# One graph-network kernel of four layers: the last V groups of each layer in one go, V one score group sooner in layer 3, and two small moves on ScalarE's queue

## The chip, the cores and the metric

The kernel runs on one NeuronCore of one Trainium2 chip. The metric is the device time of one execution in microseconds (us); the median of three runs is used. The engines are named as in the profile: PE (TensorE, matmuls and transposes), PEld (its weight loads), DVE (VectorE), ACT (ScalarE), POOL (GpSimd, which here issues the indirect DMAs) and SP (SyncE, which issues plain loads). ACTq, SPq and POOLq are the queues of DMA issues of these engines.

## The reference

x is 3327 x 256 in float32, adj is a 0/1 matrix of 3327 x 3327 in which a row has some 16 ones. Layer 0 is a graph attention with one score per node, a projection and a layer norm. Layers 1 to 3 are transformer blocks whose attention is masked with adj:

```python
qkv = layer_norm(x, g1, be1) @ w_qkv                 # 256 -> 3 x 256
q, k, v = ...                                        # 8 heads of 32
scores = einsum('nhd,mhd->hnm', q, k) * 32 ** -0.5
attn = softmax(where(adj != 0, scores, -inf), axis=-1)
x = x + einsum('hnm,mhd->nhd', attn, v).reshape(n, 256) @ w_proj + b_proj
ff = gelu(layer_norm(x, g2, be2) @ w1 + b1) @ w2 + b2   # 256 -> 1024 -> 256
x = x + ff
```

## The kernel before

Layer 0 reads adj densely, and builds for each node the list of its neighbours. The nodes are sorted by their number of neighbours and cut into 26 blocks of 128 nodes. Block b has CAPS[b] slots (40 for block 0, 24 to 10 for the others); a slot is one neighbour of each of the 128 nodes. From then on attention is sparse.

**Gathers.** Each layer's keys and values lie in DRAM, one row of 512 numbers per node (`kv[L]`). For one slot of one block, POOL issues an indirect DMA that brings the 128 neighbours' rows, one to each partition (L1303 in `issue`). Four slots make a group, the unit of all attention work: 448 slots and about 120 groups per layer. Groups land in a ring of NBUF = 10 tiles. The next group is issued when V of an earlier one has been written down (`values` calls `issue`), and POOL can run it once that V has read its tile.

**Scores.** `scores` (L1325, L1326, both DVE) multiplies k with the block's q and sums over each head. After a block's last group `softmax` subtracts on DVE and takes exp on ACT (L1340). Right behind it `take_q` (L1311) copies the next block's q on ACT.

**V.** `weights` (L1346 to L1353, DVE) makes the softmax weights of a block at its first V group. `values` multiplies v by them (vw, L1366, DVE; three tiles of vw) and adds up over the slots by transposing matmuls into PSUM (L1372, eight rows of PE in the profile for each group). After a block's last V, five short steps follow (`block`): nothing, oT copied by ACT (L1390), projection on PE (L1394, L1396), nothing, residual add on DVE with the statistics for the norm (L1400).

**Chunks.** Blocks are taken in an order that alternates small and large ones, with block 0 last, and are bundled in chunks: three blocks, then fours, then one of two, and block 0 alone. When a chunk's last block is added, `chunk` puts its long steps in a list, each with a cost: norm (rsqrt of 13 small DVE rows, L551 to L582), xn on ACT (L588), transposes (L591), then `up` (L1439), `gelu` on ACT (L1445) and `down` (L1462; L1455 and L1458 for a single block), transposes back (L1476), residual adds (L1480). In layers 1 and 2 the norm and the q/k/v of the next layer follow (`qkv`, L1492), with `keep`, which copies the k/v row (kvr, L1498), scales q (L1499) and writes kvr to DRAM (L1500, ACT's DMA queue). In layer 3 `store` writes the result by an indirect DMA of POOL (L1505).

**Order.** Each engine runs its instructions in the order in which they are written. `Layer.run` writes down one score group, then one or two V groups of an earlier block, then calls `some`. It takes a short step, then long steps as far as a credit goes (raised by `rate` in each call, at most 8), then another short step. After the last score group the remaining ten V groups of block 0 are written, each followed by `some`, and at last what is left of the lists with a rate of 4.

**Between layers.** The next layer's gathers need all 26 kvr writes. In the same stretch SP loads the next layer's weights (`load_rest`, `load_qkv`), each as soon as the last matmul has read the old ones: w_proj, w1 and w2, the bias rows (which DVE splits in three, L1255 to L1259), and w_qkv of the layer after (768 KB, L619; only at the end of layer 1, since layer 3 needs no further one).

Of the kernel before, what the change touches and what calls it, by code (L numbers as in the profile page):

```python
# [8 lines left out]
FP = mybir.dt.float32  # L9
BF = mybir.dt.bfloat16  # L10
I32 = mybir.dt.int32
AF = mybir.ActivationFunctionType
# [5 lines left out]
P = 128  # L18
N = 3327
D = 256  # L20
HEADS = 8
# [502 lines left out]
def sparse_path(ctx, tc, ins, out, dram, flag):  # L524
    nc = tc.nc
    const = ctx.enter_context(tc.tile_pool(name="s_const", bufs=1))
    small = ctx.enter_context(tc.tile_pool(name="s_small", bufs=4))

    ident = const.tile([P, P], FP, name="s_ident")
# [12 lines left out]
    kv = {1: dram.tile([PADDED + 1, KVW[1]], FP, name="kv1"),  # L542
          2: dram.tile([PADDED, KVW[2]], FP, name="kv2"),
          3: dram.tile([PADDED, KVW[3]], FP, name="kv3")}
# [732 lines left out]
    class Layer:  # L1277
# [133 lines left out]
        def chunk(self, blocks, n2):  # L1411
            L, w, nxt = self.L, self.w, self.nxt
# [82 lines left out]
            def keep(j):  # L1495
                b = blocks[j]
                kvr = work.tile([P, 2 * D], FP, tag="kvr", name=f"kvr_{L}_{b}")
                nc.scalar.copy(kvr, c["pk", j])  # L1498
                nc.scalar.mul(t2[:, b, D:2 * D], c["pq", j][:, :D], -HD ** -0.5)  # L1499
                nc.scalar.dma_start(kv[L + 1][b * P:(b + 1) * P, :], kvr)  # L1500

            def store(j):
                b = blocks[j]
# [27 lines left out]
            if nxt is not None:  # L1531
                steps += [at(2, lambda: c["n1"].scale()), *(at(2, t) for t in turns("n1", "n")),
                          at(2, lambda: to_hT("n1", "n", nxt["g1"], nxt["be1"])),
                          at(3, lambda: qkv(0))]
                for j in js:
                    fs = [lambda j=j: keep(j)]
                    if j + 1 < len(blocks):
                        fs.append(lambda j=j: qkv(j + 1))
                    steps.append(at(3, *fs))
            else:  # L1540
                steps += [at(1, lambda j=j: store(j)) for j in js]
# [12 lines left out]
                self.short.pop(0)()  # L1554

        def run(self):
            for _ in range(NBUF):
                self.issue()
            self.take_q(ORDER[0])

            todo, wait = [], {}

            def value():
                if todo[0][1] == 0:
                    self.weights(todo[0][0])
                self.values(*todo.pop(0))

            for k, b in enumerate(ORDER):
                for g in slots[b]:
                    self.scores(*g)  # L1570
                    if g == slots[b][-1]:
                        self.softmax(b)
                        if k + 1 < NB:
                            self.take_q(ORDER[k + 1])
                    for i in wait:
                        wait[i] += 1
                    for _ in range(2 if len(todo) > NBUF // 2 or b == 0 else 1):
                        if todo and wait[todo[0][0]] > 1:
                            value()
                    self.some()  # L1580
                todo += slots[b]
                wait[b] = 0
            while todo:
                value()
                self.some()
            self.rate = 4.0
            while self.short or self.long:
                self.some()
# [45 lines left out]
```

## Time and profile before

| what | us |
|---|---|
| three runs, lowest to highest | 2568.12 to 2575.34 |
| median | 2573.75 |
| profiled execution, its own time | 3158.07 |
| its span | 3156.3 |
| PE, DVE, ACT, POOL busy in the span | 1794.0, 1935.3, 774.6, 1362.7 |
| layer 1: first gather to first gather of layer 2 | 509.5 to 1428.5 |
| layer 2: to first gather of layer 3 | 1428.5 to 2305.9 |
| layer 3: to the end | 2305.9 to 3156.3 |

The profiled execution is much longer than a run without the profiler. Durations of single instructions are read from it; sums of waits are not carried over to the runs without asking. "The tail" of a layer is the stretch from its last gather to the next layer's first, in which POOL has nothing to gather: the last gather of layer 2 ends at 2191.75, the next layer's first starts at 2305.85. The page's mean TensorE clock is 0.735 of full speed.

### The profile page before, as it was taken

The page shows a single profiled execution, that of the slowest core. Times are in us where ns is not written, and L with a number is a line of the kernel's source. Part 1 is how long each engine was busy: PE and PEld are TensorE (multiplying, and loading weights), DVE is VectorE, ACT ScalarE, POOL GpSimd, SP SyncE. Part 2 cuts the span into 40 slices and gives each one's busy share as a digit, 9 for nine tenths or more (in the row PEclk, how much of TensorE's full clock was granted, in tenths as well). Part 3 has the DMA queues.
Part 4 walks back from the last instruction along what each step waited for, and adds up shares of the span by engine and source line. Part 5 has one row for each costly group of instructions (what it writes and reads, how often), then busy time and mean ns, then how long its engine had stood idle before and what let it go on. Part 6 is the DMA issues. An engine that isn't in the chain of part 4 may idle for free.

```text
span 3156.3 us, 24036 instructions
## 1 busy us (share of the span) xinstructions
PE 1794.0 (57%) x7561; PEld 1163.5 (37%) x7561; DVE 1935.3 (61%) x3983; ACT 774.6 (25%) x1316; POOL 1362.7 (43%) x1458
## 2 busy tenths in 40 slices
PE   4767752255666666671457667666713435665556
PEld 3645531133333333350334333433512323433334
DVE  6688995457657656533656756755446556656554
ACT  4455621012222222230112212222300111212112
POOL 4000004545555554305555555544054555565550
PEclk9868766577787886785578778878755766776768
DMA  5334306645555565415455555555064554554560
GB/s 207 131 117 148 129 31 204 174 138 169 165 172 162 156 174 152 112 51 177 141 156 156 163 160 150 175 152 140 24 189 125 156 155 135 169 163 147 161 156 13
DMA packets 144486, 453.80 MB, mean 144 GB/s; under 512 B 29521, under 2 KB 40156, under 8 KB 141021
## 3 DMA queue, kind: packets, MB, share of 16 engines
q0 software_dynamic: 113056, 370.26, 40.9%
q1 hardware_dynamic: 9834, 53.90, 4.9%
q10 hardware_dynamic: 21458, 28.02, 2.5%
q8 instruction: 61, 1.00, 0.1%
q14 instruction: 77, 0.63, 0.1%
HBM read 420.64 MB, written 31.42 MB: 143 GB/s over the span
## 4 chain that ended last, share of the span: by engine, by line
DVE 25%; issue 18%; PE 18%; another core or an unknown queue 17%; POOL 11%; ACT 5%; DMA 5%; DVEq 0%; ACTq 0%; POOLq 0%; SPq 0%
POOL kv L1303 11%; DVE kv L1325 5%; DMA kv<-kv,t 4%; DVE sc L1326 3%; DVE vw L1366 3%; PE pu L1439 3%; PE po L1372 3%; PE py L1462 2%; DVE cand L735 2%; PE pk L1492 1%; PE s_pk L1010 1%; ACT s_aT L724 1%; DVE s_v L731 1%; PE pf L591 1%
## 5 line engine op out<-in xcount | busy, mean ns | idle before, releaser
L1303 POOL DMA_INDIRECT kv<-kv,t x1344 | 1273.0, 947 | 1210.3 <-issue 534.2
L1372 PE MATMUL po<-s_ident,vw 128*128 128x128 f32 x2688 | 475.4, 334 | 580.2 <-DVE vw L1366 387.2
L1372 PEld LDWEIGHTS po<-s_ident,vw 128*128 128x128 f32 x2688 | 395.5, 174 | 724.1 <-issue 373.5
L1325 DVE TENSOR_TENSOR kv<-kv,q 128x1024 f32<-128x1024 f32 (+3 forms) x363 | 413.1, 1138 | 397.1 <-ACT q L1311 274.6
L1366 DVE TENSOR_TENSOR vw<-kv,w 128x1024 f32<-128x1024 f32 x333 | 371.4, 1128 | 87.2 <-remote 84.6
L1326 DVE TENSOR_REDUCE sc<-kv 128x32 f32<-128x1024 f32 (+3 forms) x363 | 414.1, 1141 | 12.4
L1439 PE MATMUL pu<-fT,s_w 128*128 128x512 f32 (+3 forms) x768 | 341.2, 579 | 62.3 <-issue 35.8
L1462 PE MATMUL py<-gT,s_w 128*128 128x512 f32 (+2 forms) x672 | 321.8, 597 | 58.1 <-issue 50.2
L1400 DVE TENSOR_TENSOR t<-t,po 128x256 f32<-128x256 f32 x78 | 32.6, 418 | 390.8 <-remote 254.5
L1445 ACT ACTIVATE gT<-pu,pvb 128x512 f32<-128x512 f32 (+3 forms) x192 | 115.7, 607 | 628.2 <-remote 384.1
L1439 PEld LDWEIGHTS pu<-fT,s_w 128*128 128x128 f32 x768 | 157.4, 222 | 196.1 <-issue 146.4
L1462 PEld LDWEIGHTS py<-gT,s_w 128*128 128x128 f32 x672 | 132.6, 206 | 180.7 <-issue 144.0
L1396 PEld LDWEIGHTS po<-s_w_proj,oT 128*128 128x128 f32 x312 | 71.8, 255 | 281.8 <-issue 272.3
L1394 PE MATMUL po<-bias,s_ones_bf 96*128 96x256 bf16 x78 | 25.2, 324 | 259.7 <-issue 147.4
L1390 ACT COPY oT<-po 128x256 f32<-128x256 f32 x78 | 28.9, 371 | 548.5 <-remote 320.2
L711 POOL MEMSET s_abf<- 128x1 bf16 x23 | 2.2, 104 | 361.4 <-DVE s_v L731 253.7
L1492 PE MATMUL pk<-s_w_qkv,nT 128*128 128x512 f32 x208 | 128.4, 748 | 22.0 <-ACT nT L596 9.9
L735 DVE MAX8 cand<-s_v 128x8 f32<-128x208 bf16 x416 | 118.0, 360 | 0.9
L1396 PE MATMUL po<-s_w_proj,oT 128*128 128x256 f32 x312 | 113.1, 500 | 0.0
L723 PE MATMUL s_ptb<-s_ident_bf,s_abf 128*128 128x128 bf16 x676 | 67.1, 265 | 68.3 <-ACT s_abf L714 45.2
L591 PE MATMUL pf<-s_ident,xn_f 128*128 128x128 f32 x156 | 46.1, 444 | 86.8 <-ACT xn_f L588 66.7
L855 PE MATMUL s_pa<-s_aT,s_hs 128*128 128x256 bf16 x338 | 82.3, 290 | 13.2 <-DVE s_hs L817 13.2
(288 smaller groups left out, 2252.1 us busy)
## 6 DMA issues: line engine op xcount, KB each, us to landing
s_a<-in_adj_dram SPq DMA_DIRECT2D x25, 1663.5 KB
kv<-kv,t POOLq DMA_INDIRECT x1344
kv<-kvr ACTq DMA_DIRECT2D x52, 256.0 KB
kv<-s_kvr ACTq DMA_DIRECT2D x26, 256.0 KB
s_w<-in_L_gnn_w_dram SPq DMA_DIRECT2D x6, 1024.0 KB
t<-ql ACTq DMA_DIRECT2D x6, 592.0 KB
t<-s_x ACTq DMA_DIRECT2D x6, 512.0 KB
s_w_qkv<-in_L_gnn_w_qkv_dram SPq DMA_DIRECT2D x3, 768.0 KB
```

Source lines behind the costliest of these rows:

```text
L735: nc.vector.max(out=self.cand[:, s, :], in_=self.v[:, s, :])
L855: nc.tensor.matmul(self.pa[:, c0:c0 + 2 * P], S.hs[:r, k, :P], aT[:r, k, :], start=(k == 0), stop=(k == NB - 1))
L1303: nc.gpsimd.indirect_dma_start(out=t[:, s, :], out_offset=None, in_=kv[L], in_offset=bass.IndirectOffsetOnAxis(ap=t2[:, b, k:k + 1].bitcas ...
L1325: nc.vector.tensor_mul(k, k, self.q[b][:, None, :].to_broadcast([P, n, D]))
L1326: nc.vector.tensor_reduce(self.sc[b][:, s0:s0 + n, :], k.rearrange("p s (h d) -> p s h d", d=HD), AX.X, ALU.add)
L1366: nc.vector.tensor_mul(vw[:, :n * D].rearrange("p (s h d) -> p s h d", h=HEADS, d=HD), v, self.wp[b][:, s0:s0 + n, :, None].to_broadcast([ ...
L1372: nc.tensor.matmul(self.po[b][:, k * P:(k + 1) * P], vw[:, at:at + P], ident, is_transpose=True, start=(s0 + s == 0 and k == 0), stop=(s0 ...
L1396: nc.tensor.matmul(ps, c["oT"][:, k * P:(k + 1) * P], w["w_proj"][:, k, :], start=False, stop=(k == 1))
L1439: nc.tensor.matmul(c["pu", f][:, :n], w["w1"][:, e, f * P:(f + 1) * P], c["hT"][:, e, :n], start=(e == 0), stop=(e == 1))
L1445: nc.scalar.activation(g[:, :n], c.pop(("pu", f))[:, :n], AF.Gelu_apprx_tanh, bias=w["b1"][:, f:f + 1])
L1462: nc.tensor.matmul(c["py"][e][:, :n], w["w2"][:, f, e * P:(e + 1) * P], g[:, :n], start=(f == 0), stop=last)
L1492: nc.tensor.matmul(ps[:, :c1 - c0], c["hT"][:, e, j * P:(j + 1) * P], nxt["w_qkv"][:, e, c0:c1], start=(e == 0), stop=(e == 1))
```

## The change

There are four edits, in `keep` and in `Layer.run`.

1. In `keep` the DMA that writes the k/v row to DRAM is issued before the scaling of q instead of after it.
2. In layer 3 (the one without `nxt`) a block's V may begin after one score group of the following block instead of two (`behind`).
3. After the last score group, one activation of a 128 x 8 piece of the identity with gelu is issued on ACT, into a tile that nothing reads.
4. The ten V groups that are left are written one after another without `some` between them. What was left of the long steps is written after them, in the old order, with the rate of 4; the chunks stay as they were.

```diff
@@ keep @@
                 nc.scalar.copy(kvr, c["pk", j])
+                nc.scalar.dma_start(kv[L + 1][b * P:(b + 1) * P, :], kvr)
                 nc.scalar.mul(t2[:, b, D:2 * D], c["pq", j][:, :D], -HD ** -0.5)
-                nc.scalar.dma_start(kv[L + 1][b * P:(b + 1) * P, :], kvr)
@@ Layer.run @@
+            L = self.L
...
+            behind = 2 if self.nxt else 1
...
-                        if todo and wait[todo[0][0]] > 1:
+                        if todo and wait[todo[0][0]] >= behind:
                             value()
...
+            table = small.tile([P, HEADS], FP, tag="table", name=f"table_{L}")
+            nc.scalar.activation(table, ident[:, :HEADS], AF.Gelu_apprx_tanh)
             while todo:
                 value()
-                self.some()
             self.rate = 4.0
             while self.short or self.long:
                 self.some()
```

## The prediction

> **What bounds the kernel now.** I read the page's busiest groups first, then POOL's waits, then the chain of waits and the timeline around the three layer ends, and last the table of windows for the granted clock. The page's top group is the gather of keys and values:
>
> ```profile
> L1303 POOL DMA_INDIRECT kv<-kv,t x1344 | 1273.0, 947 | 1210.3 <-issue 534.2
> ```
>
> One gather is 0.947 us busy and, in every unbroken run of them in the timeline, 0.30 us of issue: 1.25 us. A layer has 448, so 560 us; the three take 1680 us of the span. Of the 1210.3 us of idle time, 1344 x 0.30 = 403 are this issue and 116.8 + 114.1 = 231 the two layer changes; 576 us are left, in which POOL waits for a free place in the ring of ten groups. The profiled execution took 3158.07 us (span 3156.3, 1.8 us around it), the median of the three runs is 2573.75: 584 us less. So the unprofiled run has next to no such waits (576 of 584 is an inference from two totals, not a measured row). I take the layers as bound by POOL at 1.25 us a gather, until the last gather has landed, and then by the **tail** of each layer, in which POOL stands still. In the tails the profile has almost none of those waits, so a microsecond saved there is taken off the median one to one.
>
> The tail of layer 1 in the chain of waits, and three of its rows in the timeline:
>
> ```profile
> 1362.27 1.42 PE po L1372 x8
> ...
> 1391.96 4.42 PE po L1372 x40
> 1396.42 1.11 PE po L1372 x8
> ...
> 1418.80 3.20 PE pk L1492 x4
> 1422.00 0.86 PE pq L1492 x4
> 1422.90 4.91 DMA s_w_qkv<-in_L_gnn_w_qkv_dram
> ```
>
> ```profile
> 1402.85 0.60 ACT L588 ACTIVATE xn_f<-t,nm_f,rqy_f 128x256 f32<-128x256 f32 x1 [4.93 <-DVE nm_f L582]
> ...
> 1422.90 0.38 ACT L1499 ACTIVATE t<-pq 128x256 f32<-128x256 f32 x1 [0.28 <-PE pq L1492]
> 1422.91 0.39 ACTq L1500 DMA_DIRECT2D kv<-kvr  x1
> ```
>
> The exp of block 0 ends at 1356.3. V0 is transposed at 1362.3, V1 to V3 sit in gaps of the two-block chunk, V4 to V9 come only after that chunk's last q/k/v matmul (1391.96). Then comes block 0's own chain: oT, projection, add, norm (xn_f at 1402.85), its FFN and its q/k/v. The first gather of layer 2 is at 1428.53. Layer 2's tail repeats this within 0.3 us from exp to xn_f. In layer 3, V-only work is already one stretch of eight:
>
> ```profile
> 3116.22 9.23 DVE L1366 TENSOR_TENSOR vw<-kv,sc 128x1024 f32<-128x1024 f32 x8
> ```
>
> That is 1.154 us a group, DVE's pace.
>
> **What the Trainium skill says.** (1) "TensorE: Matmul & The Clock Gate", "What's actually happening": the array runs at half clock after about 3.4 us of idleness and again at full after about as long a busy stretch. The trace agrees in size: TensorE stands still from 1378.0 to 1383.4, the clock reads 0.50 in 1382 to 1384 and 1.00 from 1388; in the stretch of transposes 3116 to 3126 it stays 1.00. (2) "DMA: Bandwidth & Descriptors", "Queues, rings and completion order": SP and ACT each own a row of rings on the same 16 DMA engines, which serve the rows in turn. The trace agrees: alone, the last kvr write took 2.02 us (layer 2's end, 2300.17); beside the 768 KB of s_w_qkv, asked for in the same 0.01 us, about 4.9. (3) "SBUF — State Buffer", "Who interferes with whom": DVE and GpSimd share a port pair by an exclusive lock. It fits, but doesn't prove, that the first gather follows kvr's landing after 0.7 us in layer 1 and 3.7 in layer 2, amid DVE's bias rows both times. (4) "ScalarE: Activation LUTs", "What ACT_TABLE_LOAD costs": about 1283 ns a load; the rows at L1340 and L1445 show 1283.
>
> **The change, part by part.** Queue order is worked out from `some` and its credits.
>
> *V in one go.* When the scores end, ten V groups and a remainder of the two-block chunk are open: in layers 1 and 2 up2 to up7, down0 to down7, shift, back, norm, q/k/v; in layer 3 only up7, down5 to down7, shift, back, adds, stores. Today the remainder goes between the first V; afterwards V is first, and oT, projection and add of block 0 go among the remainder (two short steps per `some`), while block 0's chunk still follows it ("same chunks"). Layer 1, from V0's end at 1363.69:
> - V1 to V9: there are three vw tiles, so vw3 starts as V0 ends; seven vw at 1.154 = 8.08, plus 1.15 for the last transposes: 1372.92.
> - remainder: 6 up + 8 down at 0.865 = 12.1, projection 1.15: 1386.17. Last down to residual add 1.41 (1376.66 to 1378.07), adds and norm 4.68 (to 1382.75), xn, transposes and nT 2.8: 1395.06.
> - two q/k/v: TensorE is cold here, so the first pk takes the 3.20 of the row above, then 0.86, 1.72, 0.86: 1401.7. After the q copy (0.6) xn_f starts at 1402.3 instead of 1402.85: 0.55 gained. Its norm (13 small DVE rows, 2.6) is done by 1395, hidden behind those matmuls.
> - xn_f now follows matmuls by 1.2 us instead of 4.4 of idleness, so the array is warm: the twelve up matmuls, 2.93 today, become 1.3 (0.11 each, as from 1408 on), and the turn before loses 0.25: 1.8 gained.
>
> So 2.3 us each in layers 1 and 2. Layer 3: V0 ends at 3110.78; V9 at 3110.78 + 8.08 + 1.15 = 3120.0; up7, three down and the projection 4.6; last down to add 1.41; two adds 0.75: block 0's norm starts at 3126.8 instead of 3129.44: 2.65 gained. The last stores on POOL (0.97 each) go with the adds and end long before the final one. No gather is left to issue, so POOL and SP are passed by nothing else; the w_proj load of the next layer merely starts earlier.
>
> *Rows written ahead of q.* For each of 52 keeps the DMA issue (0.33 on ACT's queue) stands ahead of the q copy. The copy waits for pq anyway (0.28), so it is delayed by some 0.1, off the path except for the last. There the write goes at kvr's end, 1422.62 + 0.06, not at 1422.91: 0.2 earlier. In layer 1 that also puts it ahead of s_w_qkv, which is asked for at 1422.90: between 0.2 (still shared) and 3.1 (2.02 from issue to landing as alone). I take 2.2, and 0.2 in layer 2, where no s_w_qkv is loaded. The next thing late is POOL's start after the landing (0.7 or 3.7), unchanged on average, ±3.
>
> *gelu's table.* Nothing. In all three layers a gelu of the two-block chunk stands in ACT's queue between exp and the new instruction (the timeline has the L1445 load at 1358.91 and 3102.80), so the table is already in. The dummy, some 0.2 us, lies in ACT's idle time during V.
>
> *Layer 3, V after one score group.* No instruction is added. The added risk is DVE waiting for exp at `weights`, with score groups behind it. But `take_q` stands after exp on ACT, and the next block's first scores need q: DVE has waited for exp already. So no new wait. V frees its ring place one score group, at most 5 us of POOL, sooner. In the profile POOL's 26 ring waits of layer 3 add up as follows, and could shrink by up to 84 us (at most 5 each):
>
> ```profile
> POOL kv L1303 <- DVE vw L1366: 158.0, 26, 14.4
> ```
>
> Unprofiled there are next to none, so the gain lies between 0 and some 8; as a bound the other way, 3 lost by vw delaying score groups. I take 1.
>
> **Sum:** (2.3 + 2.2) + (2.3 + 0.2) + 2.65 + 1 = 10.65 us, of which 9.65 in the tails; 2573.75 - 10.65 = **2563**. A profiled execution, which has ring waits, could gain several tens more in layer 3.
>
> **Rivals.**
> 1. *The tail is only re-ordered* (0.27): the warm array or the head start of the write doesn't come, or the layer starts draw the longer 3.7 us. Then 0.55 x 2 + 0.4 + 2.65 = 4.15: 2569.6. For it: ahead of warmth only 0.55 us of a 46 us stretch from exp to xn_f is gained, a balance of large terms. Against it: the clock rows. A measurement of this kernel can't tell less than about 0.3% (7.7 us) from no change.
> 2. *The transposes cool the array* (0.10): if V-only work ran at half clock, a group would take the 1.92 us of the slow V3 row (1384.41), and nine take 17.3 instead of 9.2: +8.1 per layer, against gains of 2.3, 2.3 and 2.65; with the writes (2.4) and 1 taken off, +13.6: 2587, slower. It decides from 1.28 us per group on ((9.2 + 2.3) / 9), where layers 1 and 2 break even. Against it: clock 1.00 in layer 3's stretch of eight.
> 3. *Layer 3 had real ring waits* (0.15): 5 to 8 more gained, some 2556. For it: DVE's idle time before kv L1325 is mostly a wait for ACT's q. Against it: 576 of 584.
> 4. *A part does nothing*: so I hold of the table, at no price.
>
> The forecast itself has 0.48. **Numbers.** Predicted 2563. Range 2550 to 2574: rival 3 with the better landings below, rival 1 with noise above (the runs shown span 7 us). Faster by over 0.3%: the forecast, rival 3 = 0.63; same: rival 1, 0.27; slower: rival 2, 0.10.
>
> **What would show it.** In the changed profile: ten vw in a row at 1.15 us after each layer's last exp, clock 1.00 there and in block 0's up matmuls; xn_f of block 0 within 1 us of the last chunk matmul in layers 1 and 2; from exp's end to the next first gather about 67.5 us in layer 1 and 69.5 in layer 2 instead of 72; the last kvr landing 2 to 3 us after its issue in layer 1. Wrong if V takes over 1.28 us a group, if the up matmuls stay cold, or if layer 3's scores start waiting for exp at L1346.

## The result and the profile after

| | us, median | lowest to highest | runs |
|---|---|---|---|
| before (its first three runs and six beside the changed kernel) | 2570.82 | 2565.11 to 2575.34 | 9 |
| changed | 2562.78 | 2560.89 to 2568.05 | 9 |
| changed, second time (a_again) | 2564.56 | 2558.82 to 2567.80 | 12 |
| before, beside the second | 2570.49 | 2566.24 to 2574.38 | 20 |

The ratio is 0.9975 with a 95% interval of 0.9964 to 0.9987, and 0.9973 (0.9965 to 0.9982) the second time. Times the 2570.8 of before that is 6.4 us less (9.3 to 3.3), then 6.9 (9.0 to 4.6); the medians alone lie 8.0 and 5.9 us apart. Forecast were 10.65 us less and 2563. That the predicted time was met to 0.2 us is partly luck: the median of before is 3 us lower here than in its first three runs, and the gain itself was forecast at about one and a half times its measured size.

The profiled execution of the changed kernel took 2567.91 us (span 2566.1), within the range of its other runs. The last experiment, y4, ran on a chip where 20 runs of the kernel before read 3121 us, near the 3158.07 of its first profile, so y4 stands only against those 3121. The length of that first profile most likely came from where it ran, too, and not from being profiled: every other profiled execution took within 6 us of its kernel's median, and y4's profile shows the same long waits for the ring (POOL on vw: 378.3 us in y4, 372.7 in the first profile, 42.3 in the changed kernel). For that reason the kernel before is read below from the profile of e4_table_alone: before plus one idle instruction, span 2567.6.

The page's top group, in the columns of the one shown before (busy us and mean ns | idle before, with its releaser):

```profile
L1303 POOL DMA_INDIRECT kv<-kv,t x1344 | 1273.5, 948 | 642.2 <-issue 334.0
```

The gather costs the same 0.948 us. Of the idle 642.2, 403 are issue and 191 the two layer changes; 48 are left where the first profile had 576.

The tail of layer 1 in the chain of waits (start, length, what); block 0's exp ends at 1132.01:

```profile
1137.96 4.78 PE po L1372 x40
1142.78 1.09 PE po L1372 x8
...
1147.32 1.09 PE po L1372 x8
1148.41 0.87 PE pu L1439 x4
...
1169.60 3.50 PE pk L1492 x4
...
1178.51 2.52 PE pu L1439 x12
...
1193.08 3.69 PE pk L1492 x4
...
1197.41 2.19 DMA kv<-kvr
```

V is one block of work now, ended at 1148.4, before the chunk's remainder begins. Three TensorE rows behind it are long: both pk after a norm (3.50 and 3.69; the one between them takes 1.73) and block 0's up matmuls. The timeline of the same tail:

```profile
1134.60 1.28 ACT L1445 ACT_TABLE_LOAD   x1
...
1136.66 0.20 ACT L1588 ACTIVATE table<-s_ident 128x8 f32<-128x8 f32 x1
...
1139.23 8.04 DVE L1366 TENSOR_TENSOR vw<-kv,sc 128x1024 f32<-128x1024 f32 x7 [2.15 <-PE po L1372]
...
1177.63 0.44 PE L591 MATMUL pf<-s_ident,xn_f 128*128 128x128 f32 x2 [1.09 <-ACT xn_f L588]
1178.51 2.52 PE L1439 MATMUL pu<-fT,s_w 128*128 128x128 f32 x12 [0.44 <-ACT fT L596]
...
1197.41 0.33 ACTq L1499 DMA_DIRECT2D kv<-kvr  x1
1197.65 0.39 SPq L619 DMA_DIRECT2D s_w_qkv<-in_L_gnn_w_qkv_dram  x1
...
1200.51 1.43 POOL L1303 DMA_INDIRECT kv<-kv,t  x1 [94.44 <-DMA colsa<-in_L_gnn_be_dram]
```

Seven vw take 8.04 us, 1.149 each: DVE's pace, as forecast. The table load stands before the dummy, so the dummy loads nothing. The last kvr goes out 0.24 us ahead of s_w_qkv, and the first gather follows 3.1 us after it.

The tails, measured from exp's end of block 0 (us, from the timelines):

| | before (e4) | V in one go (e1) | changed | a_again | with idle transposes (x4) |
|---|---|---|---|---|---|
| layer 1: xn_f of block 0 | 45.58 | 44.35 | 44.98 | 44.44 | 42.74 |
| layer 1: last kvr issued | 65.55 | 65.04 | 65.40 | 64.89 | 59.97 |
| layer 1: next first gather | 71.05 | 70.63 | 68.50 | 68.13 | 63.07 |
| layer 2: last kvr issued | 65.98 | 65.55 | 65.22 | 65.21 | 59.97 |
| layer 2: next first gather | 71.65 | 71.23 | 70.79 | 70.78 | 65.55 |
| layer 3: V0's transposes to the end | 46.37 | 42.47 | 43.02 | 43.28 | 41.16 |

Layer 3 is counted from V0's transposes, because these start 8.6 or about 10 us after exp in kernels of every kind (8.60 in e2, 10.02 in e3).

### The profile page after: what moved, and what is told of

Read it like the earlier page. It is cut to its first block, busy times and chain, and to the rows that moved or that the text cites. A ratio compares the mean times of both kernels' runs of the same rounds, so it can differ in the third digit from the quotient of the medians.

```text
span 2566.1 us, 24045 instructions
## 1 busy us (share of the span) xinstructions
PE 1693.2 (66%) x7561; PEld 1131.8 (44%) x7561; DVE 1939.4 (76%) x3983; ACT 779.4 (30%) x1319; POOL 1362.0 (53%) x1458
## 4 chain that ended last, share of the span: by engine, by line
DMA 14%; DVE 13%; PE 12%; POOL 11%; issue 9%; ACT 2%; DVEq 0%; ACTq 0%; POOLq 0%; SPq 0%
DMA kv<-kv,t 13%; POOL kv L1303 10%; DVE kv L1325 3%; PE pu L1439 3%; DVE vw L1366 3%; DVE sc L1326 3%; PE po L1372 2%; PE py L1462 2%; PE pk L1492 2%; PE po L1396 1%; POOL out_dram L1505 1%; PE py L1455 0%; PE pq L1492 0%; DMA out_dram<-t,perm 0%; PE pn L591 0%
## 5 line engine op out<-in xcount | busy, mean ns | idle before, releaser
L1303 POOL DMA_INDIRECT kv<-kv,t x1344 | 1273.5, 948 | 642.2 <-issue 334.0
L1372 PE MATMUL po<-s_ident,vw 128*128 128x128 f32 x2688 | 456.6, 328 | 491.8 <-DVE vw L1366 490.2
L1372 PEld LDWEIGHTS po<-s_ident,vw 128*128 128x128 f32 x2688 | 381.0, 170 | 625.9 <-DVE vw L1366 522.9
L1326 DVE TENSOR_REDUCE sc<-kv 128x32 f32<-128x1024 f32 (+3 forms) x363 | 414.1, 1141 | 12.4
L1439 PE MATMUL pu<-fT,s_w 128*128 128x512 f32 (+3 forms) x768 | 325.3, 559 | 6.2 <-ACT gT L1445 3.5
L1462 PE MATMUL py<-gT,s_w 128*128 128x512 f32 (+2 forms) x672 | 283.0, 549 | 0.0
L1462 PEld LDWEIGHTS py<-gT,s_w 128*128 128x128 f32 x672 | 124.3, 192 | 98.7 <-issue 81.3
L588 ACT ACTIVATE xn_f<-t,nm_f,rqy_f 128x256 f32<-128x256 f32 x78 | 43.1, 593 | 194.0 <-DVE nm_f L582 188.3
L1396 PE MATMUL po<-s_w_proj,oT 128*128 128x256 f32 x312 | 100.5, 454 | 0.0
L1340 ACT ACTIVATE sc<-sc,mx 128x120 f32<-128x120 f32 (+6 forms) x78 | 32.0, 410 | 217.1 <-DVE mx L1337 216.5
L723 PEld LDWEIGHTS <-s_abf 128*128 128x128 bf16 x676 | 57.7, 124 | 78.4 <-ACT s_abf L714 56.1
L724 ACT COPY s_aT<-s_ptb 128x896 bf16<-128x896 bf16 x104 | 82.4, 859 | 21.2 <-PE s_ptb L723 21.2
```

Source lines behind the costliest of these rows:

```text
L723: nc.tensor.transpose(pt[:, m, :], self.abf[:, k * P:(k + 1) * P], ident_bf)
L1303: nc.gpsimd.indirect_dma_start(out=t[:, s, :], out_offset=None, in_=kv[L], in_offset=bass.IndirectOffsetOnAxis(ap=t2[:, b, k:k + 1].bitcas ...
L1326: nc.vector.tensor_reduce(self.sc[b][:, s0:s0 + n, :], k.rearrange("p s (h d) -> p s h d", d=HD), AX.X, ALU.add)
L1372: nc.tensor.matmul(self.po[b][:, k * P:(k + 1) * P], vw[:, at:at + P], ident, is_transpose=True, start=(s0 + s == 0 and k == 0), stop=(s0 ...
L1396: nc.tensor.matmul(ps, c["oT"][:, k * P:(k + 1) * P], w["w_proj"][:, k, :], start=False, stop=(k == 1))
L1439: nc.tensor.matmul(c["pu", f][:, :n], w["w1"][:, e, f * P:(f + 1) * P], c["hT"][:, e, :n], start=(e == 0), stop=(e == 1))
```

## The experiments

Theory T: the gain lies in the tails. Theory R: it lies in layer 3's V one group behind exp. Microseconds in this section are the ratio and its interval times the median of before beside it.

**e1, V in one go alone.**

```diff
             while todo:
                 value()
-                self.some()
```

> The kernel before with the last V groups in one go alone (no table, old order of the kvr write, two groups behind everywhere). Theory T (the tails carry the gain: earlier V chain in all three tails, head start of the write in layer 1, layer 3's ring nothing to speak of): xn_f of block 0 some 45 us after exp's end instead of 46.5, layer 3 about 2.6 us earlier, in all 4 to 6 us faster than before, so 2565 to 2567 where before reads 2571. Theory R (layer 3's V one group behind frees ring places and carries most of the gain): within 2 us of before. The warm-array term of the prediction, tested again: if it is there, the twelve up matmuls of block 0 read 1.3 us; if it is not, as in the changed kernel, 2.5 to 2.9.

Measured: 0.9985 (0.9978 to 0.9993), 3.9 us less (5.7 to 1.8). That is T's 4 to 6 within the noise; R's 2 us at most lies at the very edge of the interval, and e2 decides against it. The table gives where it came from: 0.4 us at each layer change and 3 to 4 in layer 3. The up matmuls read 2.52 us, not 1.3.

**e2, layer 3's V one group behind alone.**

```diff
+            behind = 2 if self.nxt else 1
...
-                        if todo and wait[todo[0][0]] > 1:
+                        if todo and wait[todo[0][0]] >= behind:
```

> The kernel before with layer 3's V one group behind alone. Theory T: 0 to 2 us faster, nothing that a measurement can tell. Theory R: 4 to 8 us faster, and POOL's waits on vw in layer 3 gone where the kernel before has them.

Measured: 1.0001 (0.9991 to 1.0011), 0.3 us more (2.3 less to 2.8 more). Nothing. The waits of POOL in layer 3 say why; of e4, hence of the kernel before (total us, times, longest):

```profile
POOL kv L1303 <- issue: 106.9, 351, 0.3
POOL kv L1303 <- DVE s_row L1259: 97.5, 1, 97.5
POOL out_dram L1505 <- DMA out_dram<-t,perm: 37.0, 11, 9.3
...
POOL kv L1303 <- DVE vw L1366: 3.0, 10, 0.3
```

and of e2, its largest wait on vw:

```profile
POOL kv L1303 <- DVE vw L1366: 3.7, 12, 0.3
```

No wait on vw exceeds the 0.3 us that every gather spends on issue. POOL never waits for the ring in layer 3, with or without the edit; what it waits for there is the landing of its own output stores (37.0 us, of which 9.3 lie behind the last gather).

**e3, the kvr write ahead of q alone.**

```diff
+                nc.scalar.dma_start(kv[L + 1][b * P:(b + 1) * P, :], kvr)
                 nc.scalar.mul(t2[:, b, D:2 * D], c["pq", j][:, :D], -HD ** -0.5)
-                nc.scalar.dma_start(kv[L + 1][b * P:(b + 1) * P, :], kvr)
```

> The kernel before with the kvr write issued ahead of the q copy alone. Theory T: the last kvr of layer 1 lands 2 to 3 us after its issue instead of 4.9, 2 to 2.7 us faster in all. Theory R: 0 to 0.5 us. If the early issue delays the q copies of every block, 52 times 0.1 us off the path: not slower than before by more than 1 us.

Measured: 0.9994 (0.9986 to 1.0002), 1.5 us less (3.6 less to 0.5 more). From the last write's issue to layer 2's first gather it takes 3.10 us (1194.86 to 1197.96) where e4 takes 5.50 (1196.19 to 1201.69): 2.4 gained. The DMA trace shows where: the write's last packet comes 1.8 us after its issue instead of 4.2, and the gather follows that packet by 1.3 us in both. So T's head start is there, but the time alone doesn't separate T from R: layer 2's first gather to last exp was 617.3 us, against 614.5 in e4.

**e4, the table alone.**

```diff
+            table = small.tile([P, HEADS], FP, tag="table", name=f"table_{self.L}")
+            nc.scalar.activation(table, ident[:, :HEADS], AF.Gelu_apprx_tanh)
             while todo:
```

> The kernel before with the dummy gelu ahead of the last V alone; it serves as the kernel before for a profile without long stalls, if the run has one. Theories T and R: within 1.5 us of before, since a gelu of the two-block chunk has loaded the table already. Profile: T expects layer 3's waits of POOL on vw to sum to less than 3 us; R expects 8 us or more there. Time from exp's end to block 0's norm in layer 3: 2.6 us more than in the changed kernel (26.7), so 29.3; if it is 26.7, the gain of layer 3's tail did not exist.

Measured: 1.0003 (0.9995 to 1.0011), 0.8 us more (1.3 less to 2.8 more): no effect that can be seen. Exp to block 0's norm in layer 3 takes 28.3 us, against 26.7 in the changed kernel, whose V0 started 1.35 us later after exp than here (10.16 against 8.81): counted from V0 it is 19.5 against 16.5, and the gain exists.

**x1, the changed kernel without the kvr order** (the diff of e3 taken back).

> The changed kernel with the kvr write put back behind the q copy (V in one go, table, layer 3's V one group behind kept). Theory T2 (the earlier last write gains 2.5 us at layer 2's start, and most of it is given back inside layer 2, where the last exp comes 2.8 us later after the first gather than without it): 4 to 6 us faster than before, as fast as the changed kernel within 2 us, and layer 2's first gather to last exp 614 to 616 us. Theory A (the parts add up without giving back: 2.5 us of the change's 6 to 8 come from the write): 2 to 4 us faster than before only.

Measured: 0.9983 (0.9976 to 0.9990), 4.4 us less than before (6.2 to 2.6): 2.0 and 2.5 us short of the changed kernel's two measurements, where the write's head start is 2.4. The 4.4 us and layer 2's stretch of 615.1 fit T2, the difference to the changed kernel fits A. The next run decides between them.

**x2, the changed kernel without V one group behind** (the diff of e2 taken back).

> The changed kernel with layer 3's V two groups behind, as before (V in one go, kvr ahead of q, table kept). Theory T2: the same as the changed kernel within 2 us, 4 to 7 us faster than before; the 26.7 us from layer 3's exp to block 0's norm stay below the 28 to 30 of the kernel before. Theory R (V one group behind is worth several us once the tails are short): 1 to 3 us faster than before only.

Measured: 0.9965 (0.9952 to 0.9978), 9.0 us less than before (12.3 to 5.7), not worse than the changed kernel. With e2, layer 3's new rule is worth nothing that can be seen. Its layers 1 and 2 have the same instructions as the changed kernel's, the early write among them, and yet layer 2's stretch was 614.4 here and 617.8 and 617.7 in the two profiles of the changed kernel. An early write doesn't have to be given back: T2 falls.

**x3, V in one go, and the early write in block 0 alone.**

```diff
+                if b == ORDER[-1]:
+                    write()
                 nc.scalar.mul(t2[:, b, D:2 * D], c["pq", j][:, :D], -HD ** -0.5)
+                if b != ORDER[-1]:
+                    write()
```

> V in one go, and the kvr write ahead of the q copy in block 0 alone, in the old order for the other 25 blocks. If the 2.8 us that layer 2 gives back come from delayed q copies of its own blocks (the order of each keep), they are gone here: layer 2's first gather to last exp 614 to 616 us, and 6 to 7 us faster than before. If they come from the earlier start of layer 2 itself (the same work only waits elsewhere), it reads 617 to 618 us again, and 4 us faster than before.

Measured: 0.9956 (0.9939 to 0.9972), 11.3 us less (15.7 to 7.2), more than either expectation; layer 2's stretch 617.5. That stretch is long here without the order of the 25 other blocks and short in x2 with it, so that order isn't its cause, and nor need the early start be. The traces tell more. In the four profiles with 617 to 618 us (e3, both of the changed kernel, and this one) TensorE's clock falls to 0.50 some 235 us after layer 2's first gather and stays there for 17.1 us; a residual add on DVE then waits 1.4 to 1.6 us for its projection, and POOL waits 1.5 us for the ring ahead of the 220th gather. In seven others with 614 to 616 us the clock is down for 10.2 us there and both waits are missing. The long stretches of 0.50 begin 234.5 to 235.0 us after that first gather, the short ones 235.0 to 236.5, so a small shift between clock and work goes with it. Only y3 has the long one with both waits and yet 613.8 us: the clock is the likely cause, not a shown one.

**x4, TensorE kept busy in the tails.**

```diff
+            def fill(k):
+                pt = bank(f"warm_{L}_{b0}")
+                for _ in range(k):
+                    nc.tensor.transpose(pt[:, :P], ident, ident)
...
+            if len(blocks) == 2:
+                steps.append(at(0, lambda: fill(44 if nxt is not None else 30)))
+            if len(blocks) == 1 and nxt is not None:
+                steps.append(at(0, lambda: fill(34)))
             steps += [at(1, lambda j=j: add(j)) for j in js]
```

> The changed kernel with idle transposes of the identity added on TensorE where it stands still in the tails (44 or 30 after the two-block chunk's back transposes, 34 after block 0's last down in layers 1 and 2), some 0.11 us each. Theory W (the warm-array term failed because TensorE had idled for 5.4 us ahead of the last norm and came to block 0's matmuls at half clock): the last two pk of layers 1 and 2 read 1.9 us instead of 3.5 to 3.7, the twelve up matmuls 1.3 instead of 2.5 in layers 1 and 2 and 2.9 in layer 3, so 3.2 + 1.2 us in each of layers 1 and 2 and 1.6 in layer 3, in all 8 to 10 us below the changed kernel: 13 to 17 us faster than before. Rival: the up matmuls are as slow whatever TensorE did before, so 6 us or less below the changed kernel; or the added transposes push real work back, then not below it.

Measured: 2550.94 us, 0.9922 (0.9906 to 0.9937), 20.1 us less than before (24.2 to 16.2), 12 below the changed kernel by the medians: more than the 8 to 10 expected. The timeline of layer 1's tail in x4:

```profile
1164.24 4.97 PE L1481 MATMUL warm<-s_ident 128*128 128x128 f32 x44
...
1171.28 1.98 PE L1497 MATMUL pk<-s_w_qkv,nT 128*128 128x512 f32 x4 [0.55 <-ACT nT L596]
...
1178.67 2.01 PE L1439 MATMUL pu<-fT,s_w 128*128 128x128 f32 x12 [0.44 <-ACT fT L596]
...
1191.74 1.98 PE L1497 MATMUL pk<-s_w_qkv,nT 128*128 128x512 f32 x4 [0.44 <-ACT nT L596]
```

The 44 and 34 added transposes end before the norm they stand beside. Each pk falls from 3.50 and 3.69 to 1.98, the ups from 2.52 to 2.01; the last kvr goes out 4.9 us (layer 1) and 5.2 (layer 2) earlier than in a_again, and the three tails together are 12.4 us shorter, which is the gain. The clock reads 1.00 from 1140.5 to 1198.5, where it fell three times in the changed kernel's tail before the last kvr. So the clock was the cost. The ups gained less than expected: at full clock they need 2.0, not 1.3, because two waits for ACT lie among them, one for the second half of fT and one, some 0.2 us, for the first gelu.

**y1, buffers of their own for the bias rows.**

```diff
-        room = work.tile([P, 2 * D], FP, tag="kvr", name=f"s_row_{L}")
+        room = one.tile([P, 2 * D], FP, tag="row", name=f"s_row_{L}")
```

(and the same for s_part)

> The changed kernel with buffers of their own for the bias rows (s_row, s_part), which before shared the two buffers of kvr and so waited for the last kvr's landing. The profile shows the first gather 3.2 us after that landing in layer 2's end and 0.7 in layer 1's, with DVE's rows of s_part, bias and s_row in between. Theory P (these DVE rows hold POOL up; the write's landing itself lets it go): the rows run while block 0's q/k/v are still being made, the first gather follows the landing by 0.7 us or less at both layer ends and the first two gathers take 1.25 instead of 1.75 and 1.64 us; 3 to 4 us below the changed kernel. Rival (the landing is later than it seems, or POOL waits for something else): the gap stays, within 1 us of the changed kernel.

Measured: 0.9965 (0.9954 to 0.9976) against 0.9973 for a_again in the same set: no difference that the intervals allow to state (the median is 4.4 us lower, and 3.3 of that is layer 2's stretch, 614.4 against 617.7). The timeline at layer 2's end in y1:

```profile
1878.10 0.33 ACTq L1499 DMA_DIRECT2D kv<-kvr  x1
...
1879.24 0.28 DVE L1256 COPY bias<-s_part 1x512 bf16<-1x512 bf16 x1
1883.50 0.95 POOL L1303 DMA_INDIRECT kv<-kv,t  x1 [96.65 <-issue]
```

DVE's rows are done at 1879.52, the write's last packet ends at 1879.76, and the gather still starts at 1883.50, 5.4 us after the issue (a_again: 5.6). The rival holds: those rows don't hold the start up. They did slow the first gathers of layer 2, which follow each other by 1.73 and 1.64 us in the changed kernel and by 1.25 in y1: 0.9 us in all. What POOL waits for in layer 2's last 3.7 us stays open.

**y3, layer 3's first seven stores held to the tail.**

```diff
+                late = ORDER.index(b0) < 7
-                steps += [at(1, lambda j=j: store(j)) for j in js]
+                steps += [at(1, lambda j=j: self.held.append(lambda: store(j)) if late else store(j)) for j in js]
```

(`issue` writes three held stores at each call once all gathers are issued)

> The changed kernel with the seven output stores of layer 3's first two chunks held back to the tail, behind the last gather. Theory S (layer 3's POOL is held up by its own stores, which stand in its queue and wait for one another's landing, 37 us in all, and not by the ring; that is why V one group behind brought nothing): the gaps of 4.1 + 12 us at the first and 2 x 5.7 us at the second chunk are gone, and first gather to last exp is 8 to 20 us shorter than 624; the seven stores fit in POOL's idle tail, 3.2 us each. Rival R (layer 3 is paced by DVE, or by the ring): first gather to last exp stays within 3 us of 624. Rival Q: the held stores push the last ones, so that the 53 us from exp to the end grow by what is gained.

Measured: 2541.07 us, 0.9889 (0.9874 to 0.9903), 28.5 us less than before (32.4 to 24.9), 23.5 below a_again. Layer 3's first gather to last exp is 601.2 us instead of 624.0, and exp to the end 50.4 instead of 53.4. Theory S holds. In POOL's timeline of e4 one sees what was taken away:

```profile
2067.90 2.56 POOL L1505 DMA_INDIRECT out_dram<-t,perm  x1 [0.30 <-issue]
2070.77 0.99 POOL L1303 DMA_INDIRECT kv<-kv,t  x1 [0.30 <-DVE t L1400]
2078.83 1.00 POOL L1505 DMA_INDIRECT out_dram<-t,perm  x1 [7.07 <-DMA out_dram<-t,perm]
2081.54 0.98 POOL L1505 DMA_INDIRECT out_dram<-t,perm  x1 [1.71 <-DMA out_dram<-t,perm]
2082.83 0.99 POOL L1303 DMA_INDIRECT kv<-kv,t  x1 [0.30 <-issue]
```

The second store waits 7.07 us for the landing of the first, and all gathers written after it stand behind it.

**a_again, the changed kernel once more.**

> The changed kernel itself once more, for a second profile and more runs beside those with one part left out. If its parts do not hinder each other, it stands like the kernels that leave out the kvr order or layer 3's V one group behind: 5 to 9 us faster than before. If V one group behind in layer 3 costs something (the kernel without it read 9 us faster), 4 to 7.

Measured: 0.9973 (0.9965 to 0.9982), 6.9 us less than before: within both ranges, so it doesn't separate them; the interval of x2 overlaps it.

**y4, all that helped, together** (the diffs of x4, y1 and y3 on the changed kernel).

> The changed kernel with all that helped: idle transposes that keep TensorE's clock up in the tails (12 to 13 us below the changed kernel alone), stores of layer 3's first two chunks held to the tail (23 us), bias rows in their own buffers (1 us). If they add up, 35 to 37 us below the changed kernel's 2563 to 2565: 2527 to 2530, 41 to 43 us faster than before. If the held stores and the shorter tail of layer 3 collide (the stores need 3.2 us each in a tail that is 2 us shorter), up to 5 us less of it.

Measured: 3106.01 us against 3121.32 for before on that chip, 0.994 (0.9918 to 0.9962), 18.7 us less (25.6 to 11.9). That is less than half of the 41 to 43 expected. The tails are nearly as short as in x4: 63.80, 66.00 and 47.65 us from exp's end, 20.2 in sum less than in the first profile of before (72.21, 71.94, 53.49). That alone is about the gain measured. On that chip the gathers stop in every layer, often for 9 to 15 us at a time (in layers 2 and 3 for the ring), and the 23 us of the held stores don't show in the total; whether those waits hide them was not tested. Whether the parts add up where before takes 2570 us was not measured; the fastest kernel measured there is y3.

## Why the prediction was right, and where its sum was off

- **V at DVE's pace: right.** 1.149 us a group, 1.154 forecast; the clock reads 1.00. Rival 2 needed 1.28.
- **V ahead of the remainder, layer 3: right, a little small.** 2.65 forecast; V0's transposes to the end took 46.1 us on average in e2, e3 and e4 (45.6 to 46.4), and 42.8 in the seven profiles with V in one go and the tail otherwise as it was (42.3 to 43.3): 3.3.
- **The same, layers 1 and 2: the failed term.** The prediction put 0.55 + 1.8 there. xn_f came 1.2 us earlier (45.58 to 44.35 in e1), more than forecast, but "so the array is warm: the twelve up matmuls, 2.93 today, become 1.3" failed: 2.52, and the next turn, at full clock before, now ran at half clock too. First e4, then the changed kernel:

```profile
1177.90 2.93 PE L1439 MATMUL pu<-fT,s_w 128*128 128x128 f32 x12 [0.34 <-ACT fT L596]
1180.62 0.72 PE L1455 MATMUL py<-s_w,gT 128*128 128x256 f32 x2
```

```profile
1178.51 2.52 PE L1439 MATMUL pu<-fT,s_w 128*128 128x128 f32 x12 [0.44 <-ACT fT L596]
1180.82 1.06 PE L1455 MATMUL py<-s_w,gT 128*128 128x256 f32 x2
```

  Block 0's pk, further on, became longer as well, from 3.16 in e4 to 3.68. Together 0.5 and 0.4 us were gained instead of 2.3 and 2.3: 3.7 us of the 3.8 that the whole sum is too large. Even a warm array would have given 2.0 and not 1.3 (x4). The step wrongly took the short idle gap ahead of the ups (1.09 us) as enough. The granted clock of the changed kernel in steps of 1 us (after the length, TensorE's busy us and then PEclk) shows a fall all the same:

```profile
1175.00:1176.00 1.00, 1.00 (x5) 1.00 0.30 111
1176.00:1177.00 1.00, 0.55 (x3) 1.00 0.00 0
1177.00:1178.00 1.00, 0.37 (x2) 1.00 0.70 262
1178.00:1179.00 1.00, 0.56 (x4) 1.00 0.00 0
1179.00:1180.00 1.00, 1.00 (x7) 0.76 0.00 0
1180.00:1181.00 1.00, 1.00 (x5) 0.50 0.00 0
```

  Half-busy TensorE from 1176 to 1179, with no gap over 1.09 us, is followed by 0.50 from about 1179.5 on, in the midst of the ups. The clock's changes in this tail lie 6.8, 6.8 and 3.4 us apart (1165.9, 1172.7, 1179.5, 1182.9). That agrees with the Trainium skill, "TensorE: Matmul & The Clock Gate", "What's actually happening": activity is judged in windows of about 3.4 us that run on by themselves. The prediction had used only half of this, idleness of 3.4 us, and its own profile spoke against that: TensorE stopped at 1378.0 and the clock fell at 1380.3, 2.3 us later. x4 shows the clock to be the cost: with TensorE kept busy ahead, both pk and the ups are faster.
- **The kvr write: right.** 2.2 in layer 1 forecast, 2.4 measured (5.50 to 3.10 from issue to gather); 0.2 in layer 2, about 0.3 measured (65.98 to 65.64 in e3). Landing in 2 to 3 us held. The 4.9 us read for the write before is the row of s_w_qkv; the write's own last packet came 4.3 us after its issue in that profile. The 3 us that layer 2 sometimes takes longer are as large as this gain, so that a single profile can hide it.
- **POOL's start after the landing: unchanged, as taken,** but not for the reason offered. Counted from the write's last packet it is 1.3 to 1.5 us in layer 1 and 3.7 to 4.0 in layer 2, in every profile. The prediction pointed to "SBUF — State Buffer", "Who interferes with whom" of the Trainium skill (DVE and GpSimd share a port pair by an exclusive lock) and to DVE's bias rows. y1 moved those rows away: 3.7 us in layer 2 stayed. What fits the lock, without proving it, is smaller, the 0.9 us of the first gathers.
- **The table: right**, nothing.
- **V one group behind in layer 3: 1 forecast, nothing measured.** The reason was right (few ring waits at 2570 us) and the bound of the first profile, 84 us, did not apply. Rival 3 is out: e2's profile has no ring waits in layer 3.
- **The sum.** Measured terms: 0.5 + 2.4, 0.4 + 0.3, 3.3 and 0 make 6.9 us, against 6.4 and 6.9 measured. The forecast named 67.5 and 69.5 us from exp's end to the next first gather; the changed kernel reads 68.50 and 70.79. Rival 1 (4.15) is inside the interval of the first comparison (9.3 to 3.3), but not of the second (9.0 to 4.6); its mechanism, no warm array, was true, while the write's head start, which it doubted too, came.
- **576 of 584 us.** That the runs have few of the waits of the first profile was right, that profiling brought them on is not borne out. And "next to none" left out POOL's other work: in e4 the gathers fall behind an unbroken row of 1.25 us by 41 us in layer 1 (29 of them for its own 23 row gathers, L1263), 29 in layer 2 (waits on vw) and 52 in layer 3 (stores). y3, which holds back seven of those stores, shows that these alone were worth 23 us.

## What to carry to other kernels

Before an order is polished, look in the bounding engine's own queue for instructions that wait for something else: seven stores that stood between gathers cost more than the whole change gained. In a short serial tail, count TensorE's clock as a cost of its own: where TensorE idles beside a norm, idle transposes that end before the norm does can keep the next matmuls at full clock, as in x4. And take a baseline profile from an execution whose time agrees with the runs; if it doesn't, its long waits can't be carried over.

## What the runs showed of the hardware

- The clock of TensorE can fall to 0.50 though it never idled longer than 1.09 us, after some 3 us at about half its time busy. All changes of the clock in a profile (some 150 to 200) lie on one grid with steps of 3.413 us, to within 3 ns, and the grid lies differently against the start of each execution (its first point is at 0.42 us in e1, 1.92 in the changed kernel, 3.27 in e4).
- Where the work falls on that grid matters: in the changed kernel the step from 1176.10 to 1179.52 is 0.55 busy and the clock falls at its end; in x4 nearly the same matmuls lie across two steps that are 0.68 and 0.87 busy, and it stays at 1.00. But a step that is 0.43 busy (1186.35 to 1189.76 in the changed kernel) brings no fall at its end, the next one, at 0.16, does. Which share counts as busy was not found.
- Transposes count as work for the clock: in x4 the step from 1164.37 to 1167.79 holds nothing else, and the clock stays at 1.00.
- Indirect stores on POOL that wait for one another, with no gather written between them, follow 2.7 to 4.5 us apart in e4's stream of gathers; the first pair, with a gather between, is 10.9 us apart (2067.90 to 2078.83), and the pair right behind the last gather 10.3 (2499.61 to 2509.89).
- The first gather after a layer change starts 5.5 to 5.6 us after the last kvr write's issue in layer 1 with q ahead of the write, and 3.1 to 3.3 with the write ahead. In layer 2 it is 5.4 to 5.7 in either order, with no weights on the queues and DVE idle in y1.
